# Reordering operand sums in the deep projection of a Strassen transformer block

## Chip, cores, metric

One core of a Trainium2 chip. The time is device microseconds (us) of the core per execution. The engines are TensorE (PE in the profile, its weight loads PEld), VectorE (DVE), ScalarE (ACT), GpSimd (POOL), and SyncE (SP), whose queue issues the transfers. Each engine takes its own instructions in program order.

## The reference, cut to what matters

```python
q, k, v = layer_norm(x) @ q_w + q_b, enc @ k_w + k_b, enc @ v_w + v_b   # 16 heads of 32
out = softmax(q k^T / sqrt(32) + mask) v
hidden = out @ cproj_w + cproj_b + x
y = gelu(layer_norm(hidden, ln2_w, ln2_b) @ fc_w + fc_b)                 # 512 -> 2048
return hidden + y @ proj_w + proj_b                                      # 2048 -> 512
```

x is 8 x 256 x 512, all in float32.

## The kernel before

The 2048 tokens are four groups (g = 0 to 3) of 512. First comes the attention part, then, from about 345 us on, the MLP, one stage for each group: the fc product with gelu, then the proj product. Both use Strassen's scheme in Winograd's form: seven products of half-size blocks in place of eight, with sums of the operands before them and sums of the results behind. A matrix has quarters 11, 12, 21, 22. The left operand's sums are s3 = 11 - 21, s2 = 22 - s3, s1 = s2 + 11, s4 = 12 - s2 (A_SUMS). The right operand's are t1 = 12 - 11, t2 = 22 - t1, 12 replaced by 22 - 12, t4 = 21 - t2 (B_SUMS).

**fc.** The scheme is used at two levels: `product(k, ...)` for k = 0 to 6 is one outer product, and its seven inner products are the calls of `sub`. TensorE fills a PSUM bank, ScalarE copies the first result to u1, VectorE adds the others up, and in products 1 to 6 GpSimd adds parts into the quarters of h (L1122, the helper `add` that both engines' sums go through). Weights stand in three places; the next set is loaded (L200) when a product has read the old one.

**proj.** Let A be h, with quarters A11, A12, A21 and so on; the weight is proj_w, its quarters and sums pw. The outer sums S3, S2, S1, S4 are made by `sum_h`, four instructions each: S3 in a buffer of its own, S2 in place of A21, S1 in place of A11, S4 in place of A12. For g = 0 all seven outer products are one level deep (`proj`). For g = 1 to 3 ("deep") four of them are done with a second level, by `deep_proj`, in this order: A12 by pw 21, S2 by pw t2, S1 by pw t1, S4 by pw 22. The other three (A11 by 11, S3 by 12, A22 by t4) stay one level deep.

A second-level product needs its own four sums of the left operand, made by `h_blocks` on VectorE, with 512 numbers a partition each. S2's own sums go to a buffer `hsum`; A12's, and then three of S1's, go into the buffer of S3, so A12's can start only when TensorE has read S3. The fourth argument group of `deep_proj`, `others`, is a list of lists of pieces: the first list is emitted behind result x2 (L1457 and the lines below it), the next behind x3, then behind result parts 3, 2 and 1. The seven groups of matmuls take the operands 11, s2, s3, s1, 12, 22, s4 in turn. The sixth adds to the bank that x3 is read from, so it waits for x3. `hsum[:, 4]` takes the result of both the A12 and the S2 product.

**Right-hand sums for the second level.** `p2_sums(n)` makes the four inner sums of pw n (t1, t2, t4 in a place of tile p2, block 12 in place) and stores the three to memory (L1175). p2 has two places: t2 and 22 share the first, t1 and 21 the second; `p2_load` (L1194) brings one back. Before, 21's and t1's sums are made by VectorE in stage g = 0, and 22's and t2's in g = 1, handed out by `p2_rest`: in products 0, 1, 2 (22's four), 5, 6 (t2's first two), and behind S1's sums (t2's last two).

Behind the last products of a stage VectorE makes the next group's y sums (L219 and `split_y`, L307), and the first inner results of the next stage's product 0 need them and the PSUM banks.

Of the kernel before, what the change touches and what calls it, by code (L numbers as in the profile page):

```python
# [22 lines left out]
def tile_xattn_block(  # L23
# [192 lines left out]
    def sum_up(eng, x, table, *which):  # L216
        for i in which:
            to, a, b, op = table[i]
            eng.tensor_tensor(x[to], x[a], x[b], op)  # L219
# [103 lines left out]
    with ExitStack() as att:  # L323
# [460 lines left out]
        V, GP = nc.vector, nc.gpsimd  # L784
# [175 lines left out]
        g = 1  # L960
        begin(g, 6, 1, load_res, 0, *QUARTERS)
        begin(g, 7, 1, bias_res, 0)
        g = 2
# [6 lines left out]
        g = NG - 1  # L970
# [24 lines left out]
        def run(pieces):  # L995
            for p in pieces:
                p()
# [103 lines left out]
    with ExitStack() as mlp:  # L1101
# [8 lines left out]
        NQF = HF // 2  # L1110
# [56 lines left out]
            t = p2_place(n).rearrange("p (n c s) -> p n c s", n=3, c=HF // 2)  # L1167
            return x | {m: t[:, i] for i, m in enumerate(("t1", "t2", "t4"))}

        def p2_sums(n):  # L1170
            x = pw_blocks(n)
            for i in range(4):
                sum_up(V, x, B_SUMS, i)
                if i == 3:
                    nc.sync.dma_start(p2_dram[n], p2_place(n))  # L1175
                yield

        def p2_late():


            for i, _ in enumerate(p2_sums("22")):
                if i:
                    yield
            yield
            yield
            for i, _ in enumerate(p2_sums("t2")):
                if i < 2:
                    yield
            yield

        p2_rest = p2_late()

        def p2_load(n):
            nc.sync.dma_start(p2_place(n), p2_dram[n])  # L1194
# [8 lines left out]
        for g in range(NG):  # L1203
# [18 lines left out]
            def sum_h(which, q, eng=GP):  # L1222

                x = {n: h[n][:, :, 2 * q : 2 * q + 2, :] for n in h}
                to, a, b, op = {
                    "s3": ("s3", "11", "21", ALU.subtract),
                    "s2": ("21", "22", "s3", ALU.subtract),
                    "s1": ("11", "21", "11", ALU.add),
                    "s4": ("12", "12", "21", ALU.subtract),
                }[which]  # L1230
                add(eng, x[to], x[a], x[b], op)
# [50 lines left out]
            def product(k, *sums):  # L1282


                wt, yn = w2[g, k], QI[FC_ORDER[k][1]]
                bank = {}

                def y_of(n):
                    if n in QUARTERS:
                        return ys[g].t[:, yn, int(n[0]) - 1, ts(int(n[1]) - 1, P)]  # L1290
                    return y2s[g][:, ("t1", "t2", "t4").index(n), yn, :]

                def sub(n, w, b, first, last):
                    if first:
                        bank[n] = bank_of(n, f"pf{n}_{k}").rearrange("p i (j s) -> p (i j) s", j=2)
                    for m in range(HF // 2):
                        mm(
                            bank[n][:, m, :],
                            wt[:, QI[w], ts(m, P)],
                            y_of(b),  # L1300
                            first and m == 0,
                            last,
                        )

                def u(n):
                    return us(n, f"u{n}_{k}").rearrange("p i (j s) -> p (i j) s", j=2)

                def made(cd, n, x):
                    some_gelus()
                    if k in (3, 4) and cd != "22":  # L1310
                        norm_piece()
                    if sums[0][1] is None:
                        add(V, block(sums[0][0], cd), bank[n], x)
                        return

                    r = h["s3"][:, parts[0] % 4 // 2, parts[0] % 2 * HF // 2 :][:, : HF // 2]
                    parts[0] += 1
                    add(V, r, bank[n], x)
                    for to, base in sums:
                        add(GP, block(to, cd), block(base, cd), r)  # L1320

                sub(1, "11", "11", True, False)
                u1 = u(1)
                nc.scalar.copy(u1, bank[1])  # L1324
                if g == 1:
                    next(p2_rest)
                sub(6, "s2", "t2", True, True)
                u2 = u(2)
                add(V, u2, bank[6], u1)
                some_gelus()  # L1330
                sub(7, "s3", "12", True, False)
                u3 = u(3)
                add(V, u3, bank[7], u2)
                some_gelus()
                sub(5, "21", "t1", True, False)
                made("22", 5, u3)
                sub(1, "12", "21", False, True)
                some_gelus()
                for to, base in sums:
                    if base:  # L1340
                        add(V, block(to, "11"), bank[1], block(base, "11"))
                    else:
                        nc.scalar.copy(block(to, "11"), bank[1])
                sub(7, "22", "t4", False, True)
                made("21", 7, u2)
                sub(5, "s4", "22", False, True)
                made("12", 5, u2)
                load_w2(w2_place[g, k])


            product(0, ("21", None))
            load_next()
            product(1, ("11", "21"))
# [8 lines left out]
            product(4, ("22", "12"), ("21", "21"))  # L1362
            if g == 0:
                load_pw("21")
            if g == 1:
                p2_load("21")
            product(5, ("21", "21"))
            norm_piece()
            gelu("21", 0)
# [6 lines left out]
            deep = g > 0  # L1376
# [27 lines left out]
            def turn_next(c):  # L1404
                if g + 1 < NG:
                    ps = ps_m.tile([P, G], F32, tag="mm", name=f"pyt_{g + 1}_{c}")
                    turn_hid(ps, g + 1, c)

            def o_add(eng, b, k, x):
                o = out_quarter(b, k)  # L1410
                add(eng, o, x, o)
# [13 lines left out]
            def free(i):  # L1425

                return h["s3"][:, i // 2, i % 2 * HF // 2 :][:, : HF // 2]
# [48 lines left out]
            def as_tiles(r):  # L1476

                return r.rearrange("p c s -> p (c s)").rearrange("p (i s) -> p i s", i=2)

            if deep:  # L1480
                x_s2, pieces = h_blocks("21", *(hsum[:, i] for i in range(4)))
                run(pieces)
            for q in range(NQF):
                sum_h("s1", q, V if deep else GP)
            if g == 1:
                next(p2_rest)
            proj(bank[7], "s3", "12", True, False)
            turn_next(0)
            turn_next(1)
# [1 line left out]
            if deep:  # L1491
                x_12, pieces = h_blocks("12", *(free(i) for i in range(4)))
                run(pieces[:2])
                deep_proj(x_12, "21", hsum[:, 4], pieces[2:3], pieces[3:])
                p2_load("t1")
                o_add(V, 0, 0, as_tiles(hsum[:, 4]))
                x_s1, pieces = h_blocks("11", free(0), free(1), free(2))
                run(pieces)
            else:
                proj(bank[1], "12", "21", False, True)  # L1500
                o_add(V, 0, 0, bank[1])
            for q in range(NQF):
                sum_h("s4", q)
            turn_next(2)
            turn_next(3)
            some_pw(4)
            if deep:
                deep_proj(x_s2, "t2", hsum[:, 4])
                p2_load("22")
                add(V, u2, as_tiles(hsum[:, 4]), u1)  # L1510
            else:
                proj(bank[6], "21", "t2", True, True)
                add(V, u2, bank[6], u1)
# [13 lines left out]
            if deep:  # L1527
                x_s4, pieces = h_blocks("12", hsum[:, 0], hsum[:, 1], hsum[:, 3])
                run(pieces[:1])
                deep_proj(  # L1530
                    x_s1, "t1", free(3), pieces[1:2], pieces[2:3], pieces[3:], y_sums[:1], y_sums[1:2]
                )
                if g + 1 < NG:
                    p2_load("21")
                for b in range(2):
                    o_add(GP, b, 1, as_tiles(free(3)))
                add_us()
                deep_proj(x_s4, "22", free(0), (), (), y_sums[2:3], y_sums[3:])
                if g + 1 < NG:
                    p2_load("t2")  # L1540
                o_add(V if g + 1 == NG else GP, 0, 1, as_tiles(free(0)))
            else:
                add_us()
                some_pw(4)
                for _ in p2_sums("21"):
                    pass
                proj(bank[5], "11", "t1", True, True)
                o_add(V, 0, 1, bank[5])
                o_add(V, 1, 1, bank[5])
                for _ in p2_sums("t1"):  # L1550
                    pass
                run(y_sums)
                bank[3] = bank_of(1, "py3")
                proj(bank[3], "12", "22", True, True)
                o_add(V, 0, 1, bank[3])
# [56 lines left out]
```

## Time and profile before

| | us |
|---|---|
| median of 3 runs | 735.03 (732.45 to 736.13) |
| the profiled execution | 734.65 |
| its span, first to last instruction | 732.9 |
| mean granted TensorE clock | 0.995 of full speed |

The busy time by stage of the MLP, by windows (PE, PEld, DVE, ACT, POOL busy with counts in brackets, then granted clock, DMA share, GB/s):

```
345.00:443.00 98.00, 97.71 (x650) 91.00 (x649) 72.21 (x93) 24.68 (x49) 65.39 (x49) 1.00 0.67 247
443.00:541.00 98.00, 94.28 (x735) 91.18 (x734) 79.95 (x124) 25.29 (x56) 47.12 (x35) 0.98 0.59 221
541.00:635.00 94.00, 91.99 (x730) 88.92 (x729) 72.22 (x114) 25.30 (x56) 45.80 (x35) 1.00 0.57 205
635.00:733.00 98.00, 91.30 (x709) 88.09 (x707) 61.14 (x100) 19.80 (x48) 41.15 (x32) 0.98 0.33 119
```

A matmul is two instructions in the trace (float32), so a group of four matmuls of a second-level product is listed as x8; in an undisturbed row such groups start 0.89 us apart. Instructions that were merged in a row are counted by x; the square brackets give the idle time of the engine just before and what ended it. Tiles are named without their numbers: pd is a result of `deep_proj` with pw 21 or 22, pd_t one with t1 or t2; py is one of `proj`, pf of fc; hs is S3's buffer, hsum the buffer of S2's own sums, resm the residual and output tile.

### The profile page before, as it was taken

To read this page: it belongs to the slowest core of one execution; us is meant where nothing else is said; L and a number is where in the kernel's file an instruction comes from. 1 tells how busy PE (TensorE), PEld (TensorE's weight loads), DVE (VectorE), ACT (ScalarE), POOL (GpSimd) and SP (SyncE) were. 2 spreads that over 40 slices of the span, in tenths; PEclk is the share of its full clock that TensorE was granted. 3 is DMA by queue.
4 is the path that set the end of the run, shared out by engine and by line. 5 is a ranking of instruction groups with operands and counts; after the bars stand their busy time and mean duration, and the time that the engine had idled before them with its cause. 6 is when DMAs were issued, how large, how long until landed. Compare 5 with 4: busy or idle time off the path is not lost.

```text
span 732.9 us, 14878 instructions
## 1 busy us (share of the span) xinstructions
PE 718.0 (98%) x5397; PEld 634.3 (87%) x5397; DVE 509.9 (70%) x1211; ACT 327.7 (45%) x928; POOL 477.4 (65%) x423
## 2 busy tenths in 40 slices
PE   9999999999999999999999999998999999999898
PEld 7887778887778777778998889997999989999797
DVE  3676756675456566978688588887777896766962
ACT  2277798777677787771317101253112351022300
POOL 3857899987697999886479931691335823448323
PEclk9999999999999999999999999999999999999999
DMA  9516565697639777832999215991339823393021
GB/s 303 189 59 209 201 196 192 207 314 261 227 128 303 251 259 263 285 102 87 338 396 378 94 80 200 395 374 45 130 127 398 302 92 105 127 341 120 1 87 58
DMA packets 77545, 150.68 MB, mean 206 GB/s; under 512 B 7156, under 2 KB 45344, under 8 KB 74784
## 3 DMA queue, kind: packets, MB, share of 16 engines
q1 hardware_dynamic: 77216, 149.71, 58.1%
q8 instruction: 43, 0.70, 0.4%
q14 instruction: 30, 0.25, 0.1%
q0 software_dynamic: 256, 0.02, 0.0%
HBM read 113.01 MB, written 36.70 MB: 204 GB/s over the span
## 4 chain that ended last, share of the span: by engine, by line
PE 77%; DVE 9%; DMA 6%; issue 4%; ACT 2%; POOL 1%; SPq 0%; DVEq 0%; POOLq 0%
PE pf L1119 19%; PE ppt L699 8%; PE pv L441 7%; PE pqT L441 7%; PE py L1119 5%; PE pd L1119 5%; PE po L441 5%; PE pkT L441 5%; PE s L646 5%; PE av L715 4%; PE pd_t L1119 4%; PE pkT L538 2%; DVE h L1122 2%; DMA pw<-in_L_xattn_proj_w_dram 2%; DMA w<-w_dram 2%
## 5 line engine op out<-in xcount | busy, mean ns | idle before, releaser
L1119 PEld LDWEIGHTS pf<-y,w 128*128 128x128 f32 x1568 | 175.9, 192 | 1.3 <-DVE resm L1122 0.7
L1119 PE MATMUL pf<-y,w 128*128 128x128 f32 x1568 | 176.3, 275 | 0.7 <-DVE resm L1122 0.5
L1122 POOL TENSOR_TENSOR h<-h,hs 128x512 f32<-128x512 f32 x88 | 113.3, 1308 | 93.8 <-DVE hs L1122 93.6
L688 POOL TENSOR_TENSOR pr<-pr,rsum 128x512 f32<-128x512 f32 x128 | 129.5, 1044 | 34.9 <-DVE rsum L686 24.5
L674 ACT ACTIVATE pr<-pr,nmax 128x256 f32<-128x256 f32 x256 | 127.6, 502 | 36.4 <-DVE nmax L664 36.2
L664 DVE CUSTOM_DVE_ANT_0 pr<-s,mb 128x256 f32<-128x256 f32 x256 | 93.6, 413 | 39.1 <-PE s L646 27.5
L1324 ACT COPY u<-pf 128x512 f32<-128x512 f32 x28 | 16.4, 585 | 163.7 <-PE pf L1119 163.7
L699 PEld LDWEIGHTS ppt<-ident,pr 128*128 128x128 f32 x512 | 57.3, 140 | 14.9 <-issue 5.6
L699 PE MATMUL ppt<-ident,pr 128*128 128x128 f32 x512 | 68.8, 276 | 0.3
L1122 DVE TENSOR_TENSOR hs<-pf,u 128x512 f32<-128x512 f32 x72 | 49.5, 688 | 13.4 <-PE pf L1119 12.2
L1268 ACT ACTIVATE h<-h,cols 128x256 f32<-128x256 f32 x128 | 52.0, 494 | 11.3 <-POOL h L1122 11.3
L1122 POOL TENSOR_TENSOR h<-h,h 128x512 f32<-128x512 f32 x20 | 28.0, 1425 | 43.7 <-DVE hs L1122 42.8
L1122 DVE TENSOR_TENSOR u<-pf,u 128x512 f32<-128x512 f32 x56 | 38.7, 691 | 25.0 <-PE pf L1119 21.2
L704 ACT COPY pt<-ppt 128x512 f32<-128x512 f32 x96 | 51.7, 573 | 7.1 <-PE ppt L699 7.1
L441 PE MATMUL pv<-vw,ctxT 128*128 128x256 f32 x224 | 52.4, 380 | 0.0
L441 PE MATMUL pqT<-xnT,qw 128*128 128x256 f32 x224 | 51.0, 379 | 0.0
L674 ACT ACTIVATION_READ_ACCUMULATOR pr<-pr,nmax 128x1 f32 x256 | 48.8, 191 | 0.0
L441 PEld LDWEIGHTS pqT<-xnT,qw 128*128 128x128 f32 x224 | 41.4, 190 | 5.0
L441 PEld LDWEIGHTS pv<-vw,ctxT 128*128 128x128 f32 x224 | 41.0, 190 | 5.4 <-issue 0.3
L1119 PE MATMUL py<-pw,h 128*128 128x256 f32 x192 | 42.4, 379 | 0.0
L1119 PE MATMUL py<-pw_t,h 128*128 128x256 f32 x192 | 42.3, 379 | 0.0
L1119 PEld LDWEIGHTS py<-pw_t,h 128*128 128x128 f32 x192 | 36.2, 190 | 4.7
(202 smaller groups left out, 1295.9 us busy)
## 6 DMA issues: line engine op xcount, KB each, us to landing
w<-w_dram SPq DMA_DIRECT2D x16, 1792.0 KB, 9.3
w<-in_L_xattn_fc_w_dram SPq DMA_DIRECT2D x36, 256.0 KB, 6.4
w<-w_dram SPq DMA_DIRECT2D x12, 768.0 KB, 7.5
p<-p_dram SPq DMA_DIRECT2D x6, 768.0 KB, 4.2
ctx<-in_ctx_dram SPq DMA_DIRECT2D x16, 256.0 KB, 5.1
x<-in_x_dram SPq DMA_DIRECT2D x16, 256.0 KB, 4.0
v_dram<-st_v SPq DMA_DIRECT2D x16, 256.0 KB, 2.2
v<-v_dram SPq DMA_DIRECT2D x16, 256.0 KB, 4.7
```

Of the source, the lines that this page charges most:

```text
L441: nc.tensor.matmul(bank[n][:, i, :], l[:, c, ts(i, P)], r[:, c, :], start=first and i == 0 and c == 0, stop=last and c == HC - 1, skip_gro ...
L646: nc.tensor.matmul(banks[j][:, i, :], qT[j * HD : (j + 1) * HD, b * S + i * P : b * S + (i + 1) * P], kT[j * HD : (j + 1) * HD, b * SK : ( ...
L664: nc.vector.tensor_tensor_reduce(pr[:, j, i, :], banks[j][:, i, :], mbias[g][1][:, b, :], scale=-SCALE, scalar=FLT_MAX, op0=ALU.add, op1=A ...
L674: nc.scalar.activation(pr[:, j, i, :], pr[:, j, i, :], AF.Exp, bias=nmax[:, j, i : i + 1], scale=-1.0, accum_out=sums[:, j, i : i + 1],)
L688: nc.gpsimd.tensor_tensor(pr[:, j], pr[:, j], rsum[:, j, :, None].to_broadcast([P, NQ, SK]), ALU.mult,)
L699: nc.tensor.transpose(ps[:, kc, ts(i, P)], probs[n][:, j, i, ts(kc, P)], ident)
L704: nc.scalar.copy(pt, ps)
L715: nc.tensor.matmul(av[j * HD : (j + 1) * HD, :], vs[g, hg][:, b * NK + kc, ts(j, HD)], pts[n, j][:, kc, :], start=(kc == 0), stop=(kc == N ...
L1119: nc.tensor.matmul(ps, lhsT, rhs, start=first, stop=last, skip_group_check=True)
L1122: eng.tensor_tensor(to, a, b, op)
L1268: nc.scalar.activation(h[n][:, :, p, :], h[n][:, :, p, :], AF.Gelu_apprx_tanh, bias=col(c_fcb, half * HF + p), scale=1.0,)
L1324: nc.scalar.copy(u1, bank[1])
```

## The change

Four things are changed:

- In the deep stages A12's first two own sums come straight behind S2's own on VectorE, and the four S1 sums are emitted between the results of the A12 product (one behind result 3, two behind 2, one behind 1). S1's own first two sums stay behind the A12 product, and the last two go between the results of the S2 product.
- In the deep stages the residual addition of the A12 product goes from VectorE to GpSimd, behind the four S4 sums in its order.
- The inner sums of pw 22 and 21 are made by GpSimd, all eight instructions and both stores at the start of stage g = 1. The sums of 21 by VectorE in g = 0 and the load of 21 in g = 1 are gone.
- The four t2 sums, on VectorE as before, come one each in products 3, 4, 5 and 6 of stage g = 1.

```diff
-        def p2_sums(n):
+        def p2_sums(n, eng=V):
             x = pw_blocks(n)
             for i in range(4):
-                sum_up(V, x, B_SUMS, i)
+                sum_up(eng, x, B_SUMS, i)
                 if i == 3:
                     nc.sync.dma_start(p2_dram[n], p2_place(n))
                 yield
 
-        def p2_late():
...
-        p2_rest = p2_late()
+        p2_t2 = p2_sums("t2")
...
-                if g == 1:
-                    next(p2_rest)
+                if g == 1 and k > 2:
+                    next(p2_t2)
...
+            if g == 1:
+                for n in ("22", "21"):
+                    for _ in p2_sums(n, GP):
+                        pass
             product(0, ("21", None))
...
-            if g == 1:
-                p2_load("21")
             product(5, ("21", "21"))
...
             if deep:
                 x_s2, pieces = h_blocks("21", *(hsum[:, i] for i in range(4)))
                 run(pieces)
-            for q in range(NQF):
-                sum_h("s1", q, V if deep else GP)
-            if g == 1:
-                next(p2_rest)
+                s1_sums = [lambda q=q: sum_h("s1", q, V) for q in range(NQF)]
+            else:
+                for q in range(NQF):
+                    sum_h("s1", q)
             proj(bank[7], "s3", "12", True, False)
             turn_next(0)
             turn_next(1)
             some_pw(4)
             if deep:
                 x_12, pieces = h_blocks("12", *(free(i) for i in range(4)))
                 run(pieces[:2])
-                deep_proj(x_12, "21", hsum[:, 4], pieces[2:3], pieces[3:])
+                deep_proj(
+                    x_12, "21", hsum[:, 4], pieces[2:3], pieces[3:], s1_sums[:1], s1_sums[1:3], s1_sums[3:]
+                )
                 p2_load("t1")
-                o_add(V, 0, 0, as_tiles(hsum[:, 4]))
-                x_s1, pieces = h_blocks("11", free(0), free(1), free(2))
-                run(pieces)
+                x_s1, s1_own = h_blocks("11", free(0), free(1), free(2))
+                run(s1_own[:2])
...
             for q in range(NQF):
                 sum_h("s4", q)
+            if deep:
+                o_add(GP, 0, 0, as_tiles(hsum[:, 4]))
             turn_next(2)
             turn_next(3)
             some_pw(4)
             if deep:
-                deep_proj(x_s2, "t2", hsum[:, 4])
+                deep_proj(x_s2, "t2", hsum[:, 4], (), (), s1_own[2:3], s1_own[3:])
                 p2_load("22")
                 add(V, u2, as_tiles(hsum[:, 4]), u1)
...
             else:
                 add_us()
                 some_pw(4)
-                for _ in p2_sums("21"):
-                    pass
                 proj(bank[5], "11", "t1", True, True)
```

## The prediction

> **What bounds the kernel now.** I read the page's first two parts, the waits of TensorE, the instructions of each engine in order of time in the MLP, and the granted clock there. TensorE (PE) is busy 718.0 of 732.9 us, so no change that leaves its work alone can win more than some 15 us.
>
> ```profile
> PE 718.0 (98%) x5397; PEld 634.3 (87%) x5397; DVE 509.9 (70%) x1211; ACT 327.7 (45%) x928; POOL 477.4 (65%) x423
> ```
>
> The waits of TensorE (releaser: sum, times, longest) name what there is to win. The first two rows are VectorE (DVE) being late in the three deep stages (g = 1, 2, 3), the third is the entry of g = 1:
>
> ```profile
> PE pd L1119 <- DVE hs L1122: 7.2, 4, 3.0
> ...
> PE pd_t L1119 <- DVE p L1122: 0.9, 2, 0.7
> PE pf L1119 <- DVE resm L1122: 0.5, 1, 0.5
> ...
> PE pf L1119 <- DMA w<-w_dram: 0.2, 1, 0.2
> ```
>
> The place, in order of time (start, us, engine, line, count) in stage g = 2:
>
> ```profile
> 597.55 2.49 DVE L1122 TENSOR_TENSOR h<-h,h 128x512 f32<-128x512 f32 x4
> 599.96 0.68 DVE L1122 TENSOR_TENSOR hs<-h 128x512 f32<-128x512 f32 x1
> 600.78 0.69 DVE L1122 TENSOR_TENSOR hs<-h,hs 128x512 f32<-128x512 f32 x1
> 601.52 1.16 PE L1119 MATMUL pd<-p,hs 128*128 128x128 f32 x8 [1.57 <-DVE hs L1122]
> ...
> 603.83 1.13 PE L1119 MATMUL pd<-p,hs 128*128 128x128 f32 x8 [0.25 <-DVE hs L1122]
> 603.85 5.46 POOL L1122 TENSOR_TENSOR h<-h,h 128x512 f32<-128x512 f32 x4 [13.63 <-DVE hs L1122]
> ...
> 608.07 1.79 DVE L1122 TENSOR_TENSOR resm<-hsum,resm 128x512 f32<-128x512 f32 x1
> ...
> 613.16 1.16 PE L1119 MATMUL pd_t<-p,h 128*128 128x128 f32 x8 [0.19 <-DVE p L1122]
> ```
>
> Four S1 sums (2.4 us, not needed for another product) stand ahead of the two A12 sums that the second group of the A12 product awaits. A wait costs more than its idle time. The windows of 1 us in g = 1 (PE, PEld, DVE, ACT, POOL busy, then PEclk) show the clock halved after an idle of 2.99 us:
>
> ```profile
> 505.00:506.00 1.00, 0.00 (x0) 0.00 (x0) 0.87 (x3) 0.00 (x0) 0.00 (x0) 1.00 0.00 0
> ...
> 508.00:509.00 1.00, 1.00 (x7) 1.00 (x7) 0.86 (x2) 0.00 (x0) 0.00 (x0) 0.51 0.01 0
> 509.00:510.00 1.00, 1.00 (x7) 1.00 (x6) 0.64 (x2) 0.00 (x0) 0.97 (x1) 0.50 0.00 0
> ```
>
> g = 3 shows 0.50 likewise after 2.44 us idle, g = 2 shows 1.00 after 1.57 us. From that group to the end of the product takes 7.11, 5.95 and 7.10 us in g = 1, 2, 3 (506.71 to 513.82, 601.52 to 607.47, 695.54 to 702.64), so one halving costs 1.15 us.
>
> **The A12 product.** New: the pair of A12 sums needs only the end of the S3 projection (501.95, 598.19, 692.22, by start plus duration of its row) and takes 1.5 us plus 0.05 to release TensorE. The second group (call its start T) can begin at 503.56, 599.78, and 693.85, where TensorE is free at 503.56, 599.78 and 692.94. The old T were 506.71, 601.52, 695.54. The stall goes wholly in g = 1, 2 and leaves 0.9 in g = 3. In g = 1 the two sums of t2 (1.2 us) are out of the way too. The small stall at 603.83 stays, as A12's third sum still follows the second result.
>
> **Where the S1 sums go.** They are now between results, and there GpSimd (POOL) runs its four S4 sums. A DVE sum with both operands in SBUF that meets a GpSimd sum waits for it: the residual add at 608.07 took 1.79 us and ended 0.55 after GpSimd's row ended (609.31), against 0.6 to 0.69 undisturbed. The row 489.64 (four sums, 5.71 us, GpSimd busy to 494.20) gives about 1.6 each, one GpSimd sum to one DVE sum in turn. GpSimd's own length is 1.25 (5.46 for four, less 0.46 for a DVE sum ahead of them). DVE results read from PSUM show no such stretch (0.69 in the fc products beside a busy POOL).
>
> The Trainium skill speaks against this part: SBUF — State Buffer, section "Who interferes with whom", says that a DVE instruction with two SBUF inputs and a GpSimd one that reads SBUF exclude each other for the whole instruction, by issue order; by it the sum is the lock chain below, whereas equal sharing of a port would stretch both a little.
>
> The chain after T, worked with these rows: x2 at 1.1, A12's third sum to 2.0, GpSimd starts 2.15, x3 to 2.3. A12's fourth sum asks at 2.2, is held by GpSimd's first sum to 3.4, ends 3.95 (in g = 3 that sum took 1.03 for the same reason). Result 3 to 4.2; S1 sum 1 is held by GpSimd's second sum (3.9 to 5.15), ends 5.65; result 2 to 5.85; S1 sums 2 and 3 are held by the third and fourth, ending 7.35 and 9.05; result 1 to 9.3; S1 sum 4 to 9.85. GpSimd's moved residual add then takes 9.8 to 11.05 (its own work, 1.25, is hidden; it must also free the buffer before result 3 of the S2 product, which is later). S1's own s3 is held and ends 11.55, s2 12.25, x2 and x3 of the S2 product 12.7.
>
> TensorE awaits that x3 at the sixth group of the S2 product: 4.95 (A12's seventh group) plus 0.89, plus 0.89 for the transposes in g = 1, 2, plus 4.46 for five groups: 11.2, and 10.3 in g = 3. So the wait comes back there: 1.5, 1.5 and 2.4 us. The S1 product then starts at T plus 12.75, plus 1.0 and 0.89 for two groups, that is T + 14.65: 518.2, 614.4, 708.5. Before: 521.02, 615.05, 709.83. Gains 2.8, 0.65, 1.3, sum **4.75**. DVE loses as much in lock waits (some 4.7 us a stage) as it gains by not standing in line.
>
> Bounds: without any lock wait x3 is at about T + 9.5, no stall, and the S1 product starts at T + 13.0 (12.1 in g = 3): gains 4.5, 2.3, 3.9, sum 10.7. At the other end the new stall halves the clock in all three stages, 3 x 1.15 less: 1.3. I take 4.75, nearest to the rows, which show alternation and no halving at 1.57 us. S1's own last two sums lie in gaps of 0.85 and 0.6 us between results of the S2 product (DVE rows in g = 2 and 3); nothing is charged, and if gaps close 1.2 us a stage is exposed, inside the low end.
>
> TensorE: Matmul & The Clock Gate, section "What's actually happening", has the halving after an idle window of about 3.4 us; the traces here have it at 2.44, so the row decides. By the page none of the new stalls would halve the clock.
>
> **proj_w's late sums.** GpSimd is idle 427.77 to 454.55, so eight sums of 1.25 (10 us) fit; the in-place one awaits TensorE's reading of the 22 quarter (ended 436.15). From 436.2 six remain and meet the four 128x896 DVE sums of the next y (rows of 1.08 alone, 1.95 and 2.04 beside GpSimd at 534 to 537). DVE is earlier by the removed four sums of 21 and the 2.07 us wait for their store, so y starts at 436.9 instead of 440.46. Alternating, y ends about 445.0, the residual add on bank 7 at 445.7, against 445.28: the entry stall grows by **0.45**. Bounds: 0.6 won (no contention, stall gone) and 1.0 lost. GpSimd ends at 447.5, 7 us before its first product sum.
>
> Behind it, one t2 sum each goes into products 3 to 6. In product 4 DVE has seven PSUM sums of 0.66, two norm pieces of 0.8 and now one more: 6.8 of 6.25 us. Slack of 1.09 before and 0.4 after hides most; cost 0 to 0.5, taken **0.2**. SP: the two stores (768 KB each) now queue behind the output stores (445.3) and ahead of the weight load, which TensorE releases at about 450; DMA moved nothing at 443 to 446. The 22 store and the 768 KB load of 21 leave the crowded stretch 456 to 490, so the DMA wait at 475.37 (0.25 plus 0.1 exposed weight load) goes: **0.35** won, bound 0.
>
> **Sum.** 4.75 - 0.45 - 0.2 + 0.35 = 4.45. The profiled execution took 734.65 us (span 732.9 and 1.75 around it); 734.65 - 4.45 = 730.2. The median of the runs is 735.03 (732.45 to 736.13), 0.4 above. Ends: 734.65 - 10.7 - 0.6 - 0.35 = 723.0, and 734.65 - 1.3 + 1.0 + 0.5 = 734.85.
>
> **Rivals.**
> *No lock waits decide* (0.20): sums slip in between GpSimd's; 734.65 - 10.7 + 0.3 = 724.3. For it: A12's fourth sum at 603.82 got through first (0.68). Against: 489.64 and 608.07.
> *The wait moves and halves the clock* (0.20): 730.2 + 3.45 = 733.7, no change. For it: 2.4 us forecast in g = 3 equals the idle that halved it before. Against: 1.5 in the others.
> *GpSimd's sums stretch* (0.10), the slower side: five GpSimd sums stand in DVE's way, in the A12 and S2 products. If each holds 1.71 us, as the bias adds at 490.78 and 492.49 did, x3 is 2.3 later, and the clock halves: 3.45 a stage, 730.2 + 10.4 = 740.6. It is slower from a hold of about 1.6. Against: 1.25 in the S4 sums of all three stages.
> *Forecast* (0.50): 728 to 733.
>
> A measurement of this kernel can tell 0.5%, 3.7 us: faster is below 731.35. Three quarters of the forecast and all of the first rival lie there, 0.57; slower takes the third rival and a little of the second's tail, 0.13; the rest, 0.30, is no change. The range 724.5 to 736 leaves out the lower half of the first rival and the third.
>
> **What would show it.** A12's second group without a stall in g = 1, 2 and under 1 us in g = 3; S1 sums of 1.3 to 1.7 us beside POOL; a stall of 1 to 2.5 us at the sixth group of the S2 product; y sums of about 2 us at 437 to 445. I am wrong if S1 sums take 0.6, if that stall is absent, or if PEclk falls to 0.5 there.

## The result, and the profile after

The changed kernel takes 732.2 us (median of 20 runs, 729.89 to 734.46) against 734.53 for the kernel before (20 runs beside it, 732.45 to 736.13). The ratio is 0.9966, with a 95% interval of 0.9954 to 0.9979: 2.3 us won by the medians, 2.5 by the ratio, clear of the noise and under half a per cent. The forecast was 730.2.

The page's first part after the change, busy time by engine:

```profile
PE 717.7 (98%) x5397; PEld 633.8 (87%) x5397; DVE 514.7 (70%) x1200; ACT 327.9 (45%) x928; POOL 501.5 (68%) x434
```

GpSimd (POOL) is busy 24.1 us more for eleven more instructions, which at 1.25 us each would be 13.8. VectorE (DVE) has eleven fewer and is busy 4.8 us *more*. That is the sign of the two standing in each other's way. The waits of TensorE (releaser: us in total, times, longest):

```profile
PE pd_t L1119 <- DVE p L1122: 4.8, 3, 2.2
PE pf L1119 <- DVE resm L1122: 2.6, 1, 2.6
...
PE pd L1119 <- DVE hs L1122: 0.7, 3, 0.2
```

The waits ahead of A12's second group (7.2 us, with one of 0.25 at the fourth group) are gone from the list; what is left in their row is 0.25 us at the fourth group in each of the three stages. Two waits have grown: the one for x3 at the sixth group of the S2 product, from 0.9 to 4.8 us, and the one at the entry of stage g = 1, from 0.5 to 2.6. Stage g = 2 in order of time (start, us, engine, line, form, idle time before and its releaser):

```profile
600.66 1.06 PE L1119 MATMUL pd<-p,hs 128*128 128x128 f32 x8
...
602.88 6.83 POOL L1122 TENSOR_TENSOR h<-h,h 128x512 f32<-128x512 f32 x4 [11.80 <-DVE hs L1122]
...
604.23 0.98 DVE L1122 TENSOR_TENSOR h<-h,h 128x512 f32<-128x512 f32 x1
...
606.02 2.56 DVE L1122 TENSOR_TENSOR h<-h,h 128x512 f32<-128x512 f32 x2
...
608.70 1.55 DVE L1122 TENSOR_TENSOR h<-h,h 128x512 f32<-128x512 f32 x1
...
609.67 1.72 POOL L1122 TENSOR_TENSOR resm<-hsum,resm 128x512 f32<-128x512 f32 x1
...
610.18 1.75 DVE L1122 TENSOR_TENSOR hs<-h 128x512 f32<-128x512 f32 x1
...
613.31 1.16 PE L1119 MATMUL pd_t<-p,h 128*128 128x128 f32 x8 [1.30 <-DVE p L1122]
```

The second A12 group follows the first (599.76) without a gap. The four S1 sums took 2.49 us together before; now they take 0.98, 2.56 for two, and 1.55, as GpSimd's four S4 sums run among them and are themselves stretched from 5.46 to 6.83. S1's own first sum (610.18) waits for GpSimd's residual addition. So x3 is late, and TensorE waits 1.30 us at the group where it waited 0.19 (1.29 in g = 1, 2.17 in g = 3).

The entry of stage g = 1 (this execution reached it 1.75 us later than the one before, first fc group at 444.65 against 442.90; the delay arose ahead of the MLP, where nothing was changed):

```profile
436.26 1.73 POOL L219 TENSOR_TENSOR pw<-pw 128x512 f32<-128x512 f32 x1 [3.39 <-PE py L1119]
...
440.74 1.55 DVE L307 TENSOR_TENSOR y<-y 128x896 f32<-128x896 f32 x1
...
442.32 2.04 DVE L307 TENSOR_TENSOR y<-y,y 128x896 f32<-128x896 f32 x1
443.37 2.12 POOL L219 TENSOR_TENSOR pw<-pw 128x512 f32<-128x512 f32 x1
444.29 2.15 DVE L307 TENSOR_TENSOR y<-y 128x896 f32<-128x896 f32 x1
...
445.45 2.11 POOL L219 TENSOR_TENSOR p<-pw,p 128x512 f32<-128x512 f32 x1
...
446.36 2.15 DVE L307 TENSOR_TENSOR y<-y,y 128x896 f32<-128x896 f32 x1
448.43 0.68 DVE L1122 TENSOR_TENSOR resm<-py,resm 128x512 f32<-128x512 f32 x1
...
449.16 1.05 PE L1119 MATMUL pf<-y,w 128*128 128x128 f32 x7 [2.57 <-DVE resm L1122]
```

GpSimd and VectorE take turns: the first of these y sums takes 1.55 us and the others 2.04 to 2.15 in place of 1.08, and TensorE waits 2.57 us for the addition that frees PSUM bank 7. In g = 3, where the new wait was 2.17 us, the clock (PEclk, the column behind the five engines) halves behind it:

```profile
705.00:706.00 1.00, 0.00 (x0) 0.00 (x0) 0.88 (x3) 0.00 (x0) 0.00 (x0) 1.00 0.00 0
...
708.00:709.00 1.00, 1.00 (x7) 1.00 (x6) 0.22 (x2) 0.00 (x0) 0.00 (x0) 0.50 0.81 184
```

**The account of the profiled executions.** From the first group behind the S3 projection (the transposes, in g = 3 the A12 product) to the start of the S1 product the three deep stages took 19.23, 17.03, 17.78 us and now take 16.29, 16.31, 16.47: 2.94, 0.72 and 1.31 won. The entry gives 2.57 - 0.49 = 2.08 back, a wait in product 5 (VectorE late for u) 0.26, and the halved clock at the start of g = 3's S1 product 0.81 (1.70 us to its second group against 0.89). The same halving took 0.75 us more just ahead of that product (1.64 us for the last group of the S2 product, 707.03 to 708.67, against 0.89), which is already inside the 1.31. The DMA wait in stage 1 (0.25, and 0.1 of exposed weight load) is gone. Sum 2.2 us; from stage 1's first fc group to the end of the span it is 290.0 - 288.05 = 1.95.

### The profile page after: what moved, and what is told of

Same layout as the page of the kernel before. It is cut to its first block, busy times and chain, and to the rows that moved or that the text cites. A ratio compares the mean times of both kernels' runs of the same rounds, so it can differ in the third digit from the quotient of the medians.

```text
span 732.7 us, 14870 instructions
## 1 busy us (share of the span) xinstructions
PE 717.7 (98%) x5397; PEld 633.8 (87%) x5397; DVE 514.7 (70%) x1200; ACT 327.9 (45%) x928; POOL 501.5 (68%) x434
## 4 chain that ended last, share of the span: by engine, by line
PE 84%; DVE 9%; issue 3%; ACT 1%; POOL 1%; DMA 1%; SPq 0%; DVEq 0%; ACTq 0%; POOLq 0%
PE pf L1119 21%; PE py L1119 9%; PE ppt L699 8%; PE pv L441 7%; PE pqT L441 7%; PE po L441 6%; PE pkT L441 5%; PE s L646 5%; PE av L715 4%; PE pd L1119 4%; PE pd_t L1119 4%; PE pkT L538 2%; DVE h L1122 2%; DVE hs L1122 2%; PE pxt L274 1%
## 5 line engine op out<-in xcount | busy, mean ns | idle before, releaser
L1122 POOL TENSOR_TENSOR h<-h,h 128x512 f32<-128x512 f32 x20 | 32.1, 1637 | 34.3 <-DVE hs L1122 34.3
```

The costliest lines, as they stand in the source:

```text
L1122: eng.tensor_tensor(to, a, b, op)
```

## The experiments

The edits are cut to their main lines and stand against the changed kernel; those of e7, e9 and e10 stand against the run that each builds on (e3, e8, e8). A line of three dots marks lines left out. The numbers behind a time are its ratio to the kernel before, run beside it, and the 95% interval.

**e1: GpSimd's sums undone (first try).** The sums of 22 and 21 go back to VectorE in their old places, the rest stays:

```diff
+        def p2_late():
+            for i, _ in enumerate(p2_sums("22")):
+                if i:
+                    yield
+            yield from p2_sums("t2")
...
-            if g == 1:
-                for n in ("22", "21"):
-                    for _ in p2_sums(n, GP):
-                        pass
...
+                for _ in p2_sums("21"):
+                    pass
```

> The inner sums of pw 22 and 21 go back to VectorE (22's in products 0 to 2 of stage 1, 21's in stage 0 with its load), t2's stay in products 3 to 6; the deep stages are as changed. Theory: GpSimd's eight sums cost about 2.1 us at the entry of stage 1 by holding the y sums, so the wait there falls from 2.57 to about 0.5 us, the deep stages keep their gain of about 4 us, and the time is 1.5 to 2.5 us below the changed kernel's (about 730 against 732.2; before 734.5). Rival (the entry wait is not GpSimd's doing, y is late for its own reasons): the wait stays above 2 us and the time at 732.

Measured: 736.3 us, ratio 1.0033 (1.0022 to 1.0044). The entry wait is back at 0.49, as the theory has it, but a wait of 5.92 us appears in product 3, released by VectorE's u: t2's first sum writes where 22's sums lie and stands in VectorE's queue for 7.44 us until their store has landed. The experiment asked two things at once; e5 asks the first alone. It does show what 22's early sums are good for: without them t2's sums cannot come in product 3.

**e2: the p2 part alone**, with the deep stages in the order of before.

```diff
-                s1_sums = [lambda q=q: sum_h("s1", q, V) for q in range(NQF)]
...
+            for q in range(NQF):
+                sum_h("s1", q, V if deep else GP)
...
+                deep_proj(x_12, "21", hsum[:, 4], pieces[2:3], pieces[3:])
                 p2_load("t1")
...
+                o_add(V, 0, 0, as_tiles(hsum[:, 4]))
+                x_s1, pieces = h_blocks("11", free(0), free(1), free(2))
+                run(pieces)
```

> Only the p2 part of the change: GpSimd makes 22's and 21's sums as stage 1 begins, t2's are in products 3 to 6; the order in the deep stages is that of before. Theory: the entry wait is about 2.6 us, the waits at the second group of the A12 product are 1.8 (stage 1, two t2 sums of 0.6 less in front), 1.6 and 2.4 us; plus 2.1, minus 1.2 to 2.4 with one clock halving less, so 734 to 736, no change from before. Rival (this part is what gained 2.3 us): about 732.

Measured: 735.24 us, 1.0014 (1.0003 to 1.0026); entry wait 2.58, A12's second group 2.08, 1.57 and 2.44. This part does not pay by itself. Its waits of 2.58, 2.08 and 2.44 us left the clock at full speed in the profiled run.

**e3: GpSimd's sums held until y is done.** The lock was inferred from durations; this moves the same sums out of the way. `False` takes the stores out of `p2_sums`.

```diff
             if g == 1:
+                gate = work.tile([P, 4], F32, tag="gate", name="gate")
+                add(GP, gate, y2[:, 2, 6, :4], y2[:, 2, 6, 4:8])
                 for n in ("22", "21"):
-                    for _ in p2_sums(n, GP):
+                    for _ in p2_sums(n, GP, False):
                         pass
             product(0, ("21", None))
             load_next()
+            if g == 1:
+                nc.sync.dma_start(p2_dram["22"], p2_place("22"))
             product(1, ("11", "21"))
+            if g == 1:
+                nc.sync.dma_start(p2_dram["21"], p2_place("21"))
```

> As changed, but one small GpSimd addition that reads the last y sum stands in front of GpSimd's eight sums, and their stores are issued behind the weight loads of products 0 and 1. Theory: the y sums take 0.6 and 1.1 us again instead of 1.2 and 2.1, the entry wait falls from 2.57 to under 0.3 us, GpSimd's sums run at 1.25 us each beside the PSUM sums of product 0, and the time falls by 2 to 3 us to about 729.5. Rival (GpSimd is needed early, its first product sum then comes late and VectorE waits for it): a new wait in products 1 and 2, time 731 or more.

Measured: 730.63 us, 0.9960 (0.9945 to 0.9976). Its entry, same columns:

```profile
437.36 1.09 DVE L307 TENSOR_TENSOR y<-y,y 128x896 f32<-128x896 f32 x1
438.37 1.08 DVE L307 TENSOR_TENSOR y<-y 128x896 f32<-128x896 f32 x1
439.37 1.08 DVE L307 TENSOR_TENSOR y<-y,y 128x896 f32<-128x896 f32 x1
440.53 0.20 POOL L1122 TENSOR_TENSOR gate<-y 128x4 f32<-128x4 f32 x1 [13.32 <-DVE y L307]
440.69 1.26 POOL L219 TENSOR_TENSOR p<-pw 128x512 f32<-128x512 f32 x1
...
475.69 4.51 PE L1119 MATMUL pf<-y,w 128*128 128x128 f32 x38 [1.92 <-DMA w<-w_dram]
```

The y sums take 1.08 again, GpSimd's 1.26 beside VectorE's PSUM additions, and the entry wait is gone. But the wait turned into one for a weight load, 1.92 us: both stores are now issued at 451 to 456, where the DMA moves 370 to 430 GB/s until 481. Neither theory had that, and by the ratio e3 is no faster than the changed kernel (0.9960 against 0.9966).

**e4: GpSimd's residual addition and S4 sums held** behind S1's own second sum.

```diff
+            if deep:
+                held = work.tile([P, 4], F32, tag="held", name=f"held_{g}")
+                add(GP, held, free(1)[:, 0, :4], free(1)[:, 0, 4:8])
+                o_add(GP, 0, 0, as_tiles(hsum[:, 4]))
             for q in range(NQF):
                 sum_h("s4", q)
-            if deep:
-                o_add(GP, 0, 0, as_tiles(hsum[:, 4]))
```

> As changed, but in the deep stages GpSimd's residual addition and then its four S4 sums are held behind S1's own second sum by one small addition that reads it. Theory: the S1 sums between the results take 0.6 us each instead of 1.0 to 1.75, the wait for x3 at the sixth group of the S2 product falls from 1.3, 1.3 and 2.2 to under 0.4 us each, no clock halving there, and the time falls by 4 to 6 us to 726 to 728; S4's own sums may come up to 1 us late in the S1 product. Rival (the VectorE work between the results is too long by itself): waits of 1 us or more stay at that place with sums of 0.6 us, time 731 to 733.

Measured: 729.43 us, 0.9937 (0.9924 to 0.9950). In g = 1 of e4:

```profile
509.52 0.68 DVE L1122 TENSOR_TENSOR h<-h,h 128x512 f32<-128x512 f32 x1
...
511.31 1.28 DVE L1122 TENSOR_TENSOR h<-h,h 128x512 f32<-128x512 f32 x2
...
513.31 0.68 DVE L1122 TENSOR_TENSOR hs<-h 128x512 f32<-128x512 f32 x1
...
516.17 6.30 POOL L1122 TENSOR_TENSOR h<-h,h 128x512 f32<-128x512 f32 x4
...
524.07 1.16 PE L1119 MATMUL pd_t<-p,h 128*128 128x128 f32 x8 [0.52 <-DVE p L1122]
```

All S1 sums are at 0.6 to 0.7 us and no wait is left in the S2 product: the VectorE work there was not too long by itself, it was held. GpSimd's sums now meet the sums behind the S2 product, and waits of 0.52, 0.53 and 1.40 appear one product later. The gain is 2.1 us against the changed kernel by the ratios (0.9966 - 0.9937 = 0.0029), where 4 to 6 were expected. The waits tell why: 4.76 us are gone and 2.45 have come, where the expectation allowed for up to 1 us late.

**e5: the deep part alone**, t2's sums two each in products 5 and 6, behind the landed store.

```diff
...
+            t2 = p2_sums("t2")
+            for _ in range(2):
+                next(t2)
+                next(t2)
+                yield
...
```

> The deep stages as changed; the inner sums of 22 and 21 on VectorE at the places of before, t2's four sums two each in products 5 and 6, behind the landed store of 22 (e1 had t2's first sum wait 5.9 us for that store, which hid what was asked). Theory: the entry wait is about 0.5 us, the deep stages keep their gain of some 4 us, VectorE is up to 0.5 us late in product 6, so 1.5 to 2.5 us below the changed kernel, about 730 to 731 (ratio to before 0.994 to 0.996). Rival (the deep part by itself gains no more than the whole change): 732 or more.

Measured: 731.29 us, 0.9968 (0.9956 to 0.9980). The entry wait is 0.50 and the deep stages as in the changed kernel (1.29, 1.29, 2.16), but VectorE's two sums a product cost waits of 1.21 and 0.57 us in products 5 and 6. The deep part alone gains 0.32% (0.20 to 0.44), no more than the whole change and less than expected. An estimate: without these two waits it would be some 1.8 us more.

**e6: the residual addition back on VectorE.**

```diff
+                o_add(V, 0, 0, as_tiles(hsum[:, 4]))
                 x_s1, s1_own = h_blocks("11", free(0), free(1), free(2))
...
-            if deep:
-                o_add(GP, 0, 0, as_tiles(hsum[:, 4]))
```

> As changed, with the residual addition of the A12 product back on VectorE in front of S1's own sums. Theory: GpSimd no longer holds S1's own first sum (1.75 becomes 0.68), but VectorE has one more sum (0.6 to 0.7, GpSimd's S4 sums mostly done by then), so the wait for x3 at the sixth group of the S2 product changes by less than 0.6 us a stage from 1.3, 1.3, 2.2 and the time is within 1.5 us of the changed kernel's. Rival (moving the addition to GpSimd is what freed the deep stages): waits of 2 us or more there, time back to before's 734.

Measured: 728.96 us, 0.9937 (0.9923 to 0.9951), faster than the changed kernel. In g = 2:

```profile
607.02 0.68 DVE L1122 TENSOR_TENSOR resm<-hsum,resm 128x512 f32<-128x512 f32 x1
607.62 0.68 DVE L1122 TENSOR_TENSOR hs<-h 128x512 f32<-128x512 f32 x1
...
609.68 1.16 PE L1119 MATMUL pd_t<-p,h 128*128 128x128 f32 x8 [0.83 <-DVE p L1122]
```

The addition costs VectorE 0.6 us; on GpSimd it cost VectorE 1.1 (1.75 against 0.68 for S1's own first sum). Taking work off VectorE made VectorE later. The waits fall from 1.3, 1.3, 2.2 to 0.83, 0.83, 1.70, and four of its six runs show a clock of 1.000, against eight of twenty of the changed kernel. The waits changed as little as expected (under 0.6 us a stage), the time by more than the 1.5 us expected.

**e7: e3 with the store of 21 behind product 6.**

```diff
             product(1, ("11", "21"))
-            if g == 1:
-                nc.sync.dma_start(p2_dram["21"], p2_place("21"))
...
             product(6, ("12", "12"))
+            if g == 1:
+                nc.sync.dma_start(p2_dram["21"], p2_place("21"))
```

> As e3 (GpSimd's sums behind the y sums), with the store of 21 issued behind product 6 in place of product 1. Theory: the DMA wait of 1.92 us of e3 came from two stores of 768 KB in a stretch where the DMA moved 400 GB/s; with one of them gone it falls below 0.4 us, and the time is 1 to 2 us below e3, about 729 (ratio 0.993). Rival (the weight load is late because of the store of 22 or of something else): wait 1 us or more, time as e3.

Measured: 727.65 us, 0.9921 (0.9906 to 0.9935); the DMA wait is gone, and the entry wait too. That is less than the expected 729; five of its six runs show a clock of 1.000, the profiled one among them although its g = 3 wait is 2.17 us again.

**e8: e7 and e4 together**, and S4's own first sum from ahead of the S1 product to between its results; one y sum goes from the S1 to the S4 product for it.

```diff
-                run(pieces[:1])
                 deep_proj(
-                    x_s1, "t1", free(3), pieces[1:2], pieces[2:3], pieces[3:], y_sums[:1], y_sums[1:2]
+                    x_s1, "t1", free(3), (), pieces[:1], pieces[1:2], pieces[2:3], pieces[3:] + y_sums[:1]
                 )
...
-                deep_proj(x_s4, "22", free(0), (), (), y_sums[2:3], y_sums[3:])
+                deep_proj(x_s4, "22", free(0), (), y_sums[1:2], y_sums[2:3], y_sums[3:])
```

> e7 and e4 together (GpSimd's p2 sums behind the y sums, the store of 21 behind product 6, residual addition and S4 sums behind S1's own second sum), and S4's own first sum from ahead of the S1 product to between its results. Theory: all waits that the change brought or left are gone but 0.25 us at the fourth group of each A12 product and under 0.5 us in the S1 products: about 5 us of e4's gain and 3 of e7's, 725 to 727 (ratio 0.986 to 0.989). Rival (each wait only moves on to the next VectorE sum): waits of 1 us or more in the S1 or S4 products, time 729 or more.

Measured: 722.59 us, 0.9854 (0.9835 to 0.9873). The waits of TensorE in e8:

```profile
PE pd L1119 <- DVE hs L1122: 0.8, 3, 0.3
...
PE pf L1119 <- DVE u L1122: 0.3, 1, 0.3
```

This is below the expected 725 to 727. An estimate that fits: the changed kernel's runs at a clock of 1.000 have a median of 730.25 us, and without its waits of 4.76 us for x3 and 2.57 at the entry that is 722.9.

**e9: e8 with A12's third own sum behind its second**, ahead of x2.

```diff
-                run(pieces[:2])
+                run(pieces[:3])
...
-                    x_12, "21", hsum[:, 4], pieces[2:3], pieces[3:], s1_sums[:1], s1_sums[1:3], s1_sums[3:]
+                    x_12, "21", hsum[:, 4], (), pieces[3:], s1_sums[:1], s1_sums[1:3], s1_sums[3:]
```

> As e8, with A12's third own sum straight behind its second, ahead of result x2. Theory: the 0.25 us wait at the fourth group of each A12 product (0.35 with the exposed weight load) goes in all three stages, so 1 us below e8, about 721.5 (ratio 0.984). Rival (the x2 sum then comes late and holds a later group): the wait moves, time as e8 or more.

Measured: 721.24 us, 0.9835 (0.9822 to 0.9849); the wait at A12's fourth group is gone in all three stages, and nothing has taken its place.

**e10: e8 without the holding of GpSimd.**

```diff
-                held = work.tile([P, 4], F32, tag="held", name=f"held_{g}")
-                add(GP, held, free(1)[:, 0, :4], free(1)[:, 0, 4:8])
```

(and the residual addition behind the S4 sums again)

> As e8, but GpSimd's S4 sums and residual addition are not held behind S1's own second sum; S4's own first sum stays between the results of the S1 product. Theory: the holding is what frees VectorE, so the S1 sums take 1.0 to 1.75 us again and the waits of 1.3, 1.3 and 2.2 us for x3 in the S2 product are back; about 5 us above e8, 727 to 728 (as e7). Rival (moving S4's own first sum is what made e8 fast): waits gone, time 723.

Measured: 728.55 us, 0.9935 (0.9921 to 0.9948); the waits for x3 in the S2 product are back at 4.7 us in sum, 2.1 the longest. So the place of S4's first sum wins nothing without the holding. The holding without that place (e4) leaves 2.45 us of waits in the S1 product: e8 needs both.

## Why the prediction was right, and where it was off

Direction and mechanism were right in the main; the time was 2.0 us too low and the chances leaned to "faster by over 0.5%", which it was not.

- **The A12 product**: the stall at its second group was to go in g = 1 and 2 and leave 0.9 us in g = 3. It went in all three, but for 0.2 us in g = 3 (693.30, one group after 692.20 would be 693.09). In g = 3 A12's first sum started at 691.74, ahead of the end by model of the S3 projection, where the prediction waited for that end.
- **The lock chain**: right in kind, and near in size at its end. Its x3 was to release TensorE at T plus 12.75; it did at T plus 12.64, 12.65 and 12.74. S1 sums forecast at 1.5 to 1.7 us when held, measured 0.98 to 1.55; S1's own first sum 1.7, measured 1.75. The new waits were forecast at 1.5, 1.5 and 2.4 us and are 1.29, 1.30 and 2.17. The gain up to the S1 product was forecast at 2.8, 0.65 and 1.3, measured 2.94, 0.72 and 1.31. The last agreement is luck: in g = 3 the A12 product gave 0.7 us more than forecast, and the halved clock took 0.75. GpSimd's four S4 sums, forecast at 1.25 us each, took 1.71 (6.83 for four), which the third rival named as its sign; x3 was no later for it, so such a length includes GpSimd's own waiting for VectorE. e4 and e10 take the lock away and bring it back. The Trainium skill, SBUF — State Buffer, section "Who interferes with whom", which the prediction weighed against even sharing of a port, agrees with these rows in the main: one sum a turn, and at the entry 2.15 and 2.11 us for sums of 1.08 and 1.25, which one behind the other would be 2.33. That each holds the other for its whole length is thus nearly, not fully, what the rows show.
- **The entry, the step that failed**: "From 436.2 six remain and meet the four 128x896 DVE sums", an extra 0.45 us; measured 2.08. The prediction let GpSimd's in-place sum wait for the whole projection that reads the 22 quarter. It overwrites only half the row blocks, and began at 436.26, 1.6 us before that projection's end (430.83 plus 7.07). So it met the 128x512 y sums first (4.83 us for four, 2.68 before), VectorE came to the 128x896 ones 2 us late, and GpSimd was still there for all four. e3 settles that GpSimd's sums are the cause: the same sums behind y, and the wait is gone; e1, with them on VectorE, has it back at 0.49.
- **Products 3 to 6 and DMA**: 0.2 lost and 0.35 won were forecast; 0.26 (in product 5, not 4) and 0.35 came. The stores' place was luck: the prediction had them at 445.3, where the DMA moved nothing, and they were issued at 450.0 to 450.9, behind the late output stores; e3 shows a wait of 1.92 us for a place a few us later.
- **No charge for the clock**: the sum held no halving, which the second rival had at 1.15 us for each stage. The prediction itself named PEclk falling to 0.5 at the new stall as a sign of being wrong, and in g = 3 of the profiled execution it fell. One halving cost 1.64 us there (five group starts in 5.31 us, 706.04 to 711.35, against 3.67 from 613.31 to 616.98 in g = 2). The runs divide by the clock: eight of twenty show 1.000 and a median of 730.25, six show 0.998 and 732.3, six 0.994 to 0.995 and 734.0. The most frequent clock is one without a halving; the median run lies in the group of 0.998, the clock of the profiled execution with its one halving. The prediction gave this to a rival instead of adding it by its share.

In the profiled executions 4.45 us was forecast and 1.95 came. The entry (1.63 us), the halving (1.64) and product 5 (0.06) are partly balanced by some 1.0 us that the three deep stages won beyond the forecast when the halving is set apart; 0.1 us stays open. The rival with no lock waits, at 724.3, is near where e8 stands (722.59), but e8 owes that to more than the new order of VectorE's sums: the holding of GpSimd, the later store and the new place of S4's first sum are in it.

## What to carry to other kernels

In this kernel handing sums to an idle GpSimd was free only while VectorE worked from PSUM. Beside VectorE sums of two SBUF operands one GpSimd sum of 1.25 us cost VectorE 0.3 to 1.1 us, so place GpSimd's work by what VectorE does at that moment, and hold it back by a small dependency if need be (e3, e4). When a wait is removed, follow the engine that ended it to its next deadline: here 7.0 us of waits in the A12 product came back as 4.8 in the S2 product, e4 moved 2.45 on to the S1 product, and only with e8 did no wait take their place.

## What the runs showed of the hardware

- Whether a wait halves the TensorE clock depends on where it falls, and not on its length alone. The waits of 2.15 to 2.17 us in g = 3 halved it in the traces of the changed kernel, e3, e5 and e10, and not in those of e1 and e7; 2.44 us halved it in the kernel before and not in e2; 2.57 us at the entry did not halve it in the changed kernel. These two groups, of e2 and of e7, ran on at full speed:

```profile
695.08 1.16 PE L1119 MATMUL pd<-p,hs 128*128 128x128 f32 x8 [2.44 <-DVE hs L1122]
```

```profile
700.55 1.16 PE L1119 MATMUL pd_t<-p,h 128*128 128x128 f32 x8 [2.17 <-DVE p L1122]
```

- The PEclk columns show a grid behind this: a halved stretch lasts 3.41 us (707.12 to 710.53 here; in e1 two in a row, 468.31 to 475.14), and the two falls in the kernel before, at 508.03 and 695.76, are 187.73 us apart, 55 steps of 3.413. Laid through a fall of the same trace (in some the only one lies behind the last matmul), that grid cuts the entry wait of the changed kernel at 447.70 into 1.11 and 1.46 us, while the 2.17 us in g = 3 lies within one step. In the MLP of the twelve traces, with the waits of over 1 us counted, every step with 2.10 us or more of wait in it is followed by a halved one, and none with 1.68 or less is; nothing between was seen.
- The Trainium skill, TensorE: Matmul & The Clock Gate, section "What's actually happening", has the halving after an idle window of about 3.4 us and that window free-running. The grid agrees with the free-running window; a wholly idle window was not needed, 2.10 of 3.41 us was enough.
- By its clock a run of the changed kernel had none, one or two such stretches (an estimate: one takes half of 3.41 us in 732.7 off the mean, 0.0023, and the clocks are 1.000, 0.998 and 0.995). Which waits halved it in a run other than the profiled one is not shown.
- A stretched pair shows on both sides of the page: with eleven instructions fewer VectorE was busy 4.8 us more.
